# Attention scores that stay in their PSUM banks through a group, moved from key chunk to key chunk by differences of the keys

## The chip, the core and the metric

The kernel runs on one core of one Trainium2 chip. That core has five engines with instruction streams of their own: TensorE (PE in the profile, with PEld for its weight loads), VectorE (DVE), ScalarE (ACT), GpSimd (POOL) and SyncE (SP, which here only issues DMAs). Each works through its stream in order; an instruction waits on semaphores until what it needs is there, and everything behind it on that engine waits too. TensorE writes its results to PSUM, which has eight banks, each of 512 fp32 columns on 128 partitions. The metric is the device time of one execution in microseconds (us).

## What is computed

The input x has 4 sequences of 2048 rows of 256 numbers. With xn = layernorm(x), the output is

```
x + attention(xn) * silu(ffn(xn))
```

```python
q, k, v = xn @ Wq.T + bq, xn @ Wk.T + bk, xn @ Wv.T + bv   # 16 heads of 16 columns
q, k = apply_rope(q), apply_rope(k)                        # rotary positions
att = q . k / 4, masked above the diagonal, softmax over the keys
attention = (att @ v) @ Wo.T + bo
ffn = gelu(xn @ tern(W1).T + b1) @ tern(W2).T + b2          # weights rounded to -1, 0, 1
```

## The kernel before

**Tiling.** The rows are cut into 16 blocks of 512 (four to a sequence; n = block mod 4 is the place in the sequence), the heads into 4 groups of 4. So there are 64 groups (block, head group), worked through in that order. A block of place n sees n + 1 blocks of keys, that is 4(n + 1) key chunks of 128 keys. One key chunk of one group is called a unit here: 4, 8, 12 or 16 units in a group, 640 in all. Heads lie in pairs: one of a pair in partitions 0 to 63, one in 64 to 127. In each half stand 16 dimensions four times, since q and k are both split into a rounded part and a rest (`split`, lines 391 to 397, GpSimd), so that four products add up to nearly full fp32.

**One group** has three parts.

- `maxima` (line 686) takes the scores with queries as rows, 128 queries by up to 512 keys, to find each query's maximum. One step of it is two matmuls (line 704, one for each head of a pair, in two PSUM banks) and two VectorE reductions (line 727, or 731 for the short ones of the diagonal). Blocks of keys on the diagonal get a mask first (line 717). At the end the maxima are negated, turned with a matmul into two banks (line 757) and copied by ScalarE (`mT`, line 765).
- `values` (line 772) takes the scores again with keys as rows. In each unit `scores` runs for the two pairs j = 0, 1: two matmuls of k and q (line 791, part 0), two matmuls that add the negated maxima through a selector (line 791, part 1), one exponential over both banks (line 798, ScalarE), and on the four diagonal units of a group a triangular cut by GpSimd (`affine_select`, line 802). `times_v` (line 813) multiplies with the values, one unit late, so that the exponential of unit u runs beside the products of unit u - 1 with v. Line 815 issues 4 matmuls, each of which shows as two in the profile.
- `end` and `finish` divide by the sums, project, gate with the FFN and store.

**Order.** The schedule is written out by hand (lines 1067 to 1152): while group i runs its units, `maxima` of group i + 1 is advanced by `Paced.to`, half a unit's share before `scores` and half before `times_v`. So on TensorE a full unit reads: a step of maxima, scores, a step of maxima, values. `project` (line 404), which makes q, k and v of a later block, is advanced once a unit over two groups: in the blocks of place 1 and 2 over the groups 0 and 1, in those of place 3 over all four, for two blocks. `feed` (line 566, the FFN) runs at the start of one group in each block, before that group's units.

**PSUM.** Bank 7 belongs to the products with v. The seven others lie in one list (`free_banks`, line 95). `bank` takes the one that has been free longest, `two_banks` the pair of neighbours free longest, `release` puts banks back at the end. The list is worked through while the program is written, so it fixes which bank each instruction uses; on the chip the instruction then waits until the last reader of that bank is done. In `values` a pair is taken for each j and unit, and given back after the exponential.

**project** on GpSimd (on VectorE for the first two blocks): `turn` (line 474) rotates q, then k: six tensor operations and two splits of two operations each, 128 x 512 elements each. The results go to DRAM (`qd`, `kd`, four stores of 512 KB each, line 502), in the stacked order that `maxima` and `values` need. `Loads` (line 615) brings them back by SP: q in 3 buffers, k in 8, v in 5. A tile of k serves `maxima` of a group and then `values` of the same group, which gives it back after the chunk's last scores (line 830).

## Time and profile before

| what | number |
|---|---|
| time, three runs | 2402.01, 2408.93, 2418.55 us (median 2408.93) |
| profiled execution | span 2397.2 us from its first to its last instruction; the page gives no time of its own beyond that |
| median of the runs less the span | 11.7 us |
| granted TensorE clock, mean | 0.986 |
| PE / PEld / DVE / ACT / POOL busy | 95% / 51% / 68% / 61% / 37% of the span |
| DMA | 280.38 MB, mean 117 GB/s; the SP queue's packets take 35.7% of the 16 engines' time |
| line 791, products of k and q | 2560 matmuls, 554.6 us busy |
| line 791, products with the maxima | 2560 matmuls, 516.8 us busy |
| line 704, products for the maxima | 2560 matmuls, 613.0 us busy |
| line 727, reductions of 512 | 1792, 1129.6 us busy |

A matmul's time in the profile is its passage; two matmuls in the two halves of the partitions run beside each other, so how much of TensorE's stream an instruction takes is read from the distance of starts, not from its duration. A PE that is 95% busy is therefore not at its peak. The time before can be told from no change to about 1%.

### The profile page before, as it was taken

The page shows a single profiled execution, that of the slowest core. Times are in us where ns is not written, and L with a number is a line of the kernel's source. Part 1 is how long each engine was busy: PE and PEld are TensorE (multiplying, and loading weights), DVE is VectorE, ACT ScalarE, POOL GpSimd, SP SyncE. Part 2 cuts the span into 40 slices and gives each one's busy share as a digit, 9 for nine tenths or more (in the row PEclk, how much of TensorE's full clock was granted, in tenths as well). Part 3 has the DMA queues.
Part 4 walks back from the last instruction along what each step waited for, and adds up shares of the span by engine and source line. Part 5 has one row for each costly group of instructions (what it writes and reads, how often), then busy time and mean ns, then how long its engine had stood idle before and what let it go on. Part 6 is the DMA issues. An engine that isn't in the chain of part 4 may idle for free.

```text
span 2397.2 us, 43912 instructions
## 1 busy us (share of the span) xinstructions
PE 2269.8 (95%) x16852; PEld 1222.7 (51%) x16852; DVE 1620.1 (68%) x2910; ACT 1472.5 (61%) x1889; POOL 886.6 (37%) x1262
## 2 busy tenths in 40 slices
PE   5799999999999999999999999999999999999997
PEld 4554545545455455544545454455554545455443
DVE  9656677775556676696636768768663766777881
ACT  4554656656766565765766565565676646566665
POOL 2136343235443535315344542522525453431000
PEclk8889999999999999999999999999999999999998
DMA  7344335234253524234234443412514352442311
GB/s 222 113 135 161 92 127 157 58 104 136 75 165 118 178 86 159 79 91 145 67 127 128 151 142 111 155 56 86 176 58 140 120 179 79 135 140 62 88 46 32
DMA packets 247617, 280.38 MB, mean 117 GB/s; under 512 B 108784, under 2 KB 143728, under 8 KB 247408
## 3 DMA queue, kind: packets, MB, share of 16 engines
q1 hardware_dynamic: 243680, 271.95, 35.7%
q10 hardware_dynamic: 3728, 5.64, 0.7%
q8 instruction: 132, 2.16, 0.4%
q14 instruction: 77, 0.63, 0.1%
HBM read 181.08 MB, written 87.52 MB: 112 GB/s over the span
## 4 chain that ended last, share of the span: by engine, by line
PE 71%; DVE 10%; ACT 7%; POOL 6%; issue 3%; DMA 2%; SPq 1%; ACTq 0%; DVEq 0%; POOLq 0%
PE psum L791 19%; PE psum L815 19%; PE psum L704 14%; PE psum L600 5%; PE psum L513 3%; PE psum L581 3%; DVE mx L727 3%; ACT e L798 3%; DVE mx L731 2%; PE psum L539 2%; PE psum L953 2%; PE psum L717 2%; ACT mT L765 1%; POOL qklo L397 1%; ACT g L608 1%
## 5 line engine op out<-in xcount | busy, mean ns | idle before, releaser
L727 DVE TENSOR_REDUCE mx<-psum 128x1 f32<-128x512 f32 (+1 forms) x2048 | 1258.2, 666 | 497.1 <-PE psum L704 350.1
L798 ACT ACTIVATE e<-psum 128x1024 f32<-128x1024 f32 (+3 forms) x1280 | 1081.3, 894 | 630.4 <-PE psum L791 596.0
L704 PE MATMUL psum<-kst,qst 64*128 64x512 f32 (+3 forms) x2560 | 613.0, 421 | 27.1 <-ACT h L592 9.3
L815 PE MATMUL psum<-e,vg 128*32 128x512 f32 (+3 forms) x5120 | 596.5, 543 | 15.7 <-POOL e L802 15.5
L802 POOL TENSOR_SCALAR_AFFINE_SELECT e<-e 128x256 f32<-128x256 f32 x512 | 208.0, 416 | 1001.0 <-ACT e L798 972.2
L791 PE MATMUL psum<-qst,kst 64*128 64x512 f32 (+3 forms) x2560 | 554.6, 395 | 22.3 <-DVE mx L727 5.7
L704 PEld LDWEIGHTS psum<-kst,qst 64*128 64x128 f32 x2560 | 309.0, 185 | 449.4 <-DVE mx L727 287.9
L791 PE MATMUL psum<-mT,sel 64*128 64x512 f32 (+3 forms) x2560 | 516.8, 370 | 6.0 <-ACT mT L765 3.2
L791 PEld LDWEIGHTS psum<-qst,kst 64*128 64x128 f32 x2560 | 285.1, 185 | 171.9 <-ACT e L798 55.4
L791 PEld LDWEIGHTS psum<-mT,sel 64*128 64x128 f32 x2560 | 273.3, 186 | 43.7 <-ACT mT L765 24.1
L594 POOL TENSOR_TENSOR hl<-h,hh 128x512 fp32r<-128x512 f32 x128 | 164.9, 1298 | 149.9 <-ACT h L592 114.3
L815 PEld LDWEIGHTS psum<-e,vg 128*32 128x32 f32 x5120 | 109.9, 108 | 161.0 <-issue 112.4
L731 DVE TENSOR_REDUCE mx<-psum 128x3 f32<-128x384 f32 x256 | 130.3, 552 | 57.7 <-PE psum L717 53.3
L592 ACT ACTIVATE hh<-psum,b1c 128x512 fp32r<-128x512 f32 x128 | 88.4, 691 | 80.4 <-PE psum L581 80.2
L513 PE MATMUL psum<-xf,wqkvT 128*128 128x512 f32 x256 | 125.9, 616 | 0.9 <-ACT xf L458 0.9
L717 PE MATMUL psum<-mask_k,mask_q 64*128 64x64 bf16 (+1 forms) x1536 | 121.1, 205 | 0.0
L600 PE MATMUL psum<-hh,w2T 128*128 128x512 f32 x256 | 107.1, 418 | 0.2 <-ACT w2T L367 0.2
L581 PE MATMUL psum<-xh,w1T 128*128 128x512 f32 x256 | 104.8, 409 | 0.6 <-POOL xh L396 0.5
L581 PE MATMUL psum<-xl,w1T 128*128 128x512 f32 x256 | 103.1, 403 | 0.8 <-POOL xl L397 0.8
L600 PE MATMUL psum<-hl,w2T 128*128 128x512 f32 x256 | 102.3, 399 | 0.2
L521 ACT ACTIVATE qk<-psum,bqk 128x512 f32<-128x512 f32 x64 | 44.0, 689 | 86.4 <-PE psum L513 85.9
L592 ACT ACTIVATE h<-psum,b1c 128x512 f32<-128x512 f32 x128 | 87.9, 687 | 0.0
(135 smaller groups left out, 1635.9 us busy)
## 6 DMA issues: line engine op xcount, KB each, us to landing
kst<-kd SPq DMA_DIRECT2D x160, 512.0 KB
qst<-qd SPq DMA_DIRECT2D x64, 512.0 KB
vg<-vd SPq DMA_DIRECT2D x160, 166.0 KB
qd<-qkhi SPq DMA_DIRECT2D x32, 512.0 KB
qd<-qklo SPq DMA_DIRECT2D x32, 512.0 KB
kd<-qkhi SPq DMA_DIRECT2D x30, 512.0 KB
kd<-qklo SPq DMA_DIRECT2D x30, 512.0 KB
vd<-v SPq DMA_DIRECT2D x16, 574.0 KB
```

Source lines behind the costliest of these rows:

```text
L513: nc.tensor.matmul(pq, wqkvT[:, kc, at : at + P], xf[:, kc, :], start=(kc == 0), stop=(kc == KC - 1),)
L581: nc.tensor.matmul(ph, w1T[:, kc, f * P : (f + 1) * P], x12[:, kc, :], start=(kc + i == 0), stop=(kc + i == KC),)
L592: nc.scalar.activation(to, ph, AF.Gelu, bias=b1c[:, f : f + 1])
L600: nc.tensor.matmul(pgs[dc], w2T[:, f - 2, dc * P : (dc + 1) * P], hx, start=(f - 2 + i == 0), stop=(f - 2 + i == FC),)
L704: nc.tensor.matmul(s1[:, at : at + wt], q[rows, j, t * P : (t + 1) * P], kst[blk, g, c][rows, j, :wt], start=(at == 0), stop=(c < n),)
L717: nc.tensor.matmul(to[:, :, i * ST : (i + 1) * ST], mask_q[rows, i, :], mask_k[rows, i, : len(ts), :], start=False, stop=(i == 1),)
L727: nc.vector.tensor_reduce(mx[:, 2 * j + a, at : at + 1], s1[:, :w], AX.X, ALU.max)
L731: nc.vector.tensor_reduce(mx[:, 2 * j + a, at : at + w // P], s1[:, :w].rearrange("p (b k) -> p b k", k=P), AX.X, ALU.max,)
L791: nc.tensor.matmul(s2[:, a, :w], (k, sels[j][rows, :])[part], (q[rows, j, q0:], mT[rows, q0:])[part], start=(part == 0), stop=(part == 1),)
L798: nc.scalar.activation(e, s2[:, :, :w], AF.Exp, scale=1.0 / math.sqrt(HD))
L802: nc.gpsimd.affine_select(out=e[:, :, :P], in_=e[:, :, :P], pattern=[[0, 2], [1, P]], compare_op=ALU.is_ge, fill=0.0, base=0, channel_mult ...
L815: nc.tensor.matmul(av[h * HP : (h + 1) * HP, q0:], vst[blk, g, kb // TT][:, kb % TT, h * VE : h * VE + HP], ex[h // 2][:, h % 2, : NB - q0 ...
```

## The change

The scores of a pair j stay in one fixed pair of banks (0, 1 for j = 0; 2, 3 for j = 1) through all units of a group. The first unit writes the product of q and the first key chunk plus the negated maxima, as before. Each later unit adds the product of q with the differences d = (keys of this chunk) - (keys of the chunk before), which turns the scores of the one chunk into those of the next. The products with the maxima are issued in the first unit only.

- `project` makes the differences, splits them and stores them (`steps_of_keys`, four stores of 512 KB to `sd`). It has one yield more, so `N_Q` is one higher. The rotated k is kept in `turned_k` with the last 128 columns of the block before.
- The halves hi and lo now come from a pool of two buffers of half the size, one taken by q, k and d each.
- `Loads` has a fourth kind, d, with 3 buffers and one group ahead. k is used by `maxima` alone, has 4 buffers, and is given back there.

```diff
+    def pair_of_banks(name, i):
+        free_banks.remove(i)
+        free_banks.remove(i + 1)
+        taken.setdefault(name, []).append([i, i + 1])
+        return psum[:, i : i + 2, :]
...
+    turned_k = const.tile([P, 2, P + NB], F32, name="turned_k")
+    nc.gpsimd.memset(turned_k[:, :, :P], 0.0)
...
-    kp = ctx.enter_context(tc.tile_pool(name="kp", bufs=8))
+    kp = ctx.enter_context(tc.tile_pool(name="kp", bufs=4))
+    dp = ctx.enter_context(tc.tile_pool(name="dp", bufs=3))
...
+    halfp = ctx.enter_context(tc.tile_pool(name="halfp", bufs=2))
...
+        def halved(hi, lo, full):
             if not start:
-                split(hi[:, 2 * i, :], lo[:, 2 * i, :], r0, (NB,))
+                split(hi, lo, full, (NB,))
             else:
-                nc.scalar.copy(hi[:, 2 * i, :], r0)
+                nc.scalar.copy(hi, full)
+                eng.tensor_tensor(lo, full, hi.bitcast(F32), ALU.subtract)
+
+        def stacked(dd, hi, lo, rows):
             for c, src in enumerate(rows):
...
+                queue = nc.scalar if blk == 0 and dd is not qd else nc.sync
+                queue.dma_start(out=to[c], in_=src.bitcast(F32))
...
+        def steps_of_keys():
+            hi, lo = halves()
+            for s in range(2):
+                d = one.tile([P, NB], F32, tag=f"r{s}", name=f"d{s}")
+                eng.tensor_tensor(
+                    d, turned_k[:, s, P:], turned_k[:, s, :NB], ALU.subtract
+                )
+                halved(hi[:, s, :], lo[:, s, :], d)
+            if n + 1 < NQ:
+                eng.tensor_copy(turned_k[:, :, :P], turned_k[:, :, NB:])
+            else:
+                eng.memset(turned_k[:, :, :P], 0.0)
+            stacked(sd, hi, lo, (hi, lo, hi, lo))
...
             while pairs and (blk or i):
                 turn(*pairs.pop(0))
+        steps_of_keys()
+        yield
...
-            self.free = {"q": 3, "k": 8, "v": 5}
+            self.free = {"q": 3, "k": 4, "d": 3, "v": 5}
...
-            self.ahead = {"q": 2, "k": 2, "v": 1}
+            self.ahead = {"q": 2, "k": 2, "d": 1, "v": 1}
...
+        def d(self, blk, g, c):
+            t = dst[blk, g, c] = dp.tile([P, 2, NB], F32R, tag="dst", name="dst")
+            nc.sync.dma_start(
+                out=t.bitcast(F32),
+                in_=sd[blk - blk % NQ + c][2 * g : 2 * g + 2].rearrange("r p k -> p r k"),
+            )
...
+                if ts[-1] == (TT - 1 if c < n else 0) and j == GH // 2 - 1:
+                    kst.pop((blk, g, c))
+                    loads.release("k")
...
+        banks = [pair_of_banks("s2", 2 * j) for j in range(GH // 2)]
         def scores(kb, j, q0):
-            s2 = two_banks("s2")
+            s2 = banks[j]
...
-            for part in range(2):
+            for part in range(1 if kb else 2):
                 for a in range(2):
                     rows = slice(a * ST, (a + 1) * ST)
-                    k = kst[blk, g, kb // TT][rows, j, (kb % TT) * P : (kb % TT + 1) * P]
+                    d = dst[blk, g, kb // TT][rows, j, (kb % TT) * P : (kb % TT + 1) * P]
                     nc.tensor.matmul(
-                        s2[:, a, :w],
-                        (k, sels[j][rows, :])[part],
+                        s2[:, a, q0:],
+                        (d, sels[j][rows, :])[part],
                         (q[rows, j, q0:], mT[rows, q0:])[part],
-                        start=(part == 0),
-                        stop=(part == 1),
+                        start=(kb == 0 and part == 0),
+                        stop=(kb > 0 or part == 1),
+                        skip_group_check=True,
                     )
-            nc.scalar.activation(e, s2[:, :, :w], AF.Exp, scale=1.0 / math.sqrt(HD))
-            release("s2")
+            nc.scalar.activation(e, s2[:, :, q0:], AF.Exp, scale=1.0 / math.sqrt(HD))
+            if kb == last:
+                release("s2")
...
             if kb % TT == TT - 1:
-                kst.pop((blk, g, kb // TT))
-                loads.release("k")
+                dst.pop((blk, g, kb // TT))
+                loads.release("d")
```

## The prediction

> **What bounds the kernel now.** I read the page first: the busy shares, the chain that ended last, the groups.
>
> ```profile
> span 2397.2 us, 43912 instructions
> PE 2269.8 (95%) x16852; PEld 1222.7 (51%) x16852; DVE 1620.1 (68%) x2910; ACT 1472.5 (61%) x1889; POOL 886.6 (37%) x1262
> ...
> PE 71%; DVE 10%; ACT 7%; POOL 6%; issue 3%; DMA 2%; SPq 1%; ACTq 0%; DVEq 0%; POOLq 0%
> ...
> L727 DVE TENSOR_REDUCE mx<-psum 128x1 f32<-128x512 f32 (+1 forms) x2048 | 1258.2, 666 | 497.1 <-PE psum L704 350.1
> ```
>
> TensorE carries 71% of the chain; line 791, half of which goes, has 19% of the span there. VectorE comes next, and its 68% is an average, so I went to the timeline of a stretch with nothing but attention in it (a group of place 3, in the second sequence):
>
> ```profile
> 1197.52 0.50 PE L704 MATMUL psum<-kst,qst 64*128 64x512 f32 x2
> 1197.85 0.40 PE L791 MATMUL psum<-qst,kst 64*128 64x512 f32 x2
> 1198.05 2.51 DVE L727 TENSOR_REDUCE mx<-psum 128x1 f32<-128x512 f32 x4 [1.19 <-PE psum L704]
> 1198.09 0.40 PE L791 MATMUL psum<-mT,sel 64*128 64x512 f32 x2
> 1198.32 0.41 PE L791 MATMUL psum<-qst,kst 64*128 64x512 f32 x2
> 1198.55 0.41 PE L791 MATMUL psum<-mT,sel 64*128 64x512 f32 x2
> 1198.59 1.94 ACT L798 ACTIVATE e<-psum 128x1024 f32<-128x1024 f32 x2 [0.41 <-PE psum L791]
> 1198.78 0.51 PE L704 MATMUL psum<-kst,qst 64*128 64x512 f32 x2
> 1199.22 1.06 PE L815 MATMUL psum<-e,vg 128*32 128x512 f32 x8
> 1200.21 0.51 PE L704 MATMUL psum<-kst,qst 64*128 64x512 f32 x2
> 1200.58 0.50 PE L791 MATMUL psum<-qst,kst 64*128 64x512 f32 x2
> 1200.75 4.00 DVE L727 TENSOR_REDUCE mx<-psum 128x1 f32<-128x512 f32 x6 [0.19 <-PE psum L704]
> ```
>
> From scores to scores (1197.85 to 1200.58) a unit takes 2.73 us. Each pair of matmuls of line 791 holds TensorE for 0.23 us. VectorE has two steps of maxima a unit, four reductions, 2.51 us. TensorE is the bound here with VectorE 0.2 us behind; ScalarE needs 1.94.
>
> The second place is POOL's 6%. The chain of waits shows where it lies, in the second group of a block of place 1:
>
> ```profile
> 785.55 1.29 POOL qklo L397
> ...
> 804.48 1.27 POOL qklo L397
> 805.95 0.34 POOL e L802
> 806.33 1.41 PE psum L815 x8
> ```
>
> Between these lines stands nothing but GpSimd's `turn`; the triangular cuts queue behind it, and TensorE waits (the timeline puts 1.50 us of idle time ahead of the matmul at 806.33).
>
> **What goes.** In every unit but a group's first, the two pairs with the maxima: 2304 matmuls. With 0.23 us a pair of 512 columns, 0.46 a unit, there are 448 full units less 64 first ones, 384 x 0.46 = 177 us. The narrow diagonal units (0.34, 0.24, 0.20 by their starts) give 64 x 0.78 = 50. Together 227 us, 9% of the span.
>
> **What takes it back: the banks left for the maxima.** Four of seven banks now belong to `values`; three remain for the two of each step of maxima and for all else. In a ring of three, the second matmul of a step can start only when the first reduction of the step before is done. That takes 0.53 us from issue to the start of the reduction (1197.52 to 1198.05), 0.68 for the reduction (the groups by shape: 1792 of 512 columns with a mean of 683 ns; 0.63 apart when they follow closely), and some 0.06 to the next matmul (a reduction ended at 909.83 elsewhere, the weight load behind it began at 909.89): 1.27 us. In the timeline over the whole run, 447 of the 576 changed units stand between two steps of maxima. For the full ones the distance of these steps has a median of 1.38 us (middle eight tenths 1.26 to 1.65); without the 0.46 it would be 0.9 to 1.0, so the wait puts back most. Clipped at 1.27 unit by unit, these give 44 us instead of about 160; the other 129 units give their full 41. Where a unit then has no maxima it is held by ScalarE's 1.94; I take off 6. **Gain 79 us**, bounds 0 and 150 (the upper if VectorE's 2.51 were the only limit: 0.23 in each of 344 full units, 79, plus 41 and some 30 for narrow ones and first steps).
>
> On the banks that stay: the page "PSUM — Partial Sum Buffer" of the Trainium skill, in its "Summary: rules for kernel authors", advises that TensorE write a different bank from the one being read, which speaks against this change. Taken bare it would add a wait of an exponential, 0.97 us, to each of 1152 pairs. Here the first exponential ends at 1199.56, the next product for its banks is due at 1200.5; the second at 1200.53, its product due 0.23 later, so I cost this at nothing.
>
> **What is added.**
>
> - GpSimd, 14 blocks: two subtractions of 1.28 us (row of line 479), two splits of 1.04 to 1.09 and 1.28 (lines 396, 397) and a copy of 256 elements (0.4 by the triangular cut's row, 0.7 by half a subtraction): 7.9 us, issued straight behind k's `turn`. In the place shown above nothing hides it: 4 x 7.9, and what TensorE gained in that group is lost in the wait, 3 more: **35 us**. In blocks of place 2 GpSimd idles 4.57 us before the next cut, so some 2 us stick out; in place 3's last group 9.4 us of idle time are cut down by the faster units, some 3 to 4 us stick out: together **17**. Bounds of all GpSimd terms 25 and 70.
> - `mT`. The two banks of line 757 now belong to the three. The next step of maxima comes right behind it 47 times of 64, takes one of these banks, and waits for ScalarE's copy; before, only the product with the maxima waited, with that step and the first product in the gap:
>
> ```profile
> 1217.19 0.43 PE L757 MATMUL psum<-id_half,m_pad 64*68 64x64 f32 x8
> 1217.46 0.47 PE L704 MATMUL psum<-kst,qst 64*128 64x512 f32 x2
> 1217.85 0.48 PE L791 MATMUL psum<-qst,kst 64*128 64x512 f32 x2
> 1217.89 0.57 ACT L765 CAST mT<-psum 68x512 fp32r<-68x512 f32 x1
> 1218.51 0.50 PE L791 MATMUL psum<-mT,sel 64*128 64x512 f32 x2 [0.18 <-ACT mT L765]
> ```
>
>   0.34 + 0.23 us of cover, 47 times: **27 us**, bounds 0 and 36.
> - Two steps of maxima back to back (some 16 a sequence, 0.2 to 0.9 us apart now) are pushed to 1.27. Most lie in groups where VectorE is 85 to 88% busy and would end no sooner; I count a third, 5 us a sequence: **20**, bounds 0 and 60.
> - `project` keeps one bank for v over a yield, one or two units long; then the maxima have two banks and the second matmul waits for the second reduction, 0.63 more, some 6 units a sequence outside the GpSimd wait: **14**, bounds 0 and 25.
> - SP and DMA: 160 loads and 64 stores of 512 KB, 280 to about 398 MB. SP is in order, so loads behind the d stores wait for GpSimd. The first d tile of a new sequence is released 8 units before use, behind those stores: 3 us, three times, **10**, bounds 0 and 40. Other d tiles are asked for 8 units (20 us) ahead and hide; k has a group's time.
> - Start: 3.1 us of VectorE (five operations of about 0.69 to 0.3) for each of blocks 0 and 1, and four more DMA issues on ScalarE: **6**, bounds 2 and 10.
>
> The sum: 79 - 35 - 17 - 27 - 20 - 14 - 10 - 6 = -50. The span goes from 2397 to about 2447; with the 11.7 us between span and median, 2459. The waits hide a little in one another, so I say **2455 us**, 1.9% slower.
>
> **The rivals.**
>
> 1. *Faster: VectorE becomes the bound, and the three banks don't bind.* For it: seven banks, of which four were nearly always with the scores, held up the maxima's weight loads already (287.9 us of such waits, mostly behind work that had to be done anyway), so three may be as good. Then the gain is 150, the steps back to back and the v banks cost nothing, and GpSimd 52, `mT` 0 to 27, loads 10 and start 6 remain: 55 to 82 us faster, about 2340. It decides from a distance of steps around the scores below about 1.15 us: each 0.1 there is worth some 40 us.
> 2. *No difference.* The gain is nearer 100 and a third of the waits lie in each other's shade: 2409, within 1%.
> 3. *Much slower: lockstep.* TensorE waits for VectorE at every second step, VectorE then for TensorE, which is in order and stuck behind values; back-to-back steps cost 60, the v banks 25, the loads 40, GpSimd 70: gain 60 less 231, some 2560 at the far end, 2510 as its near edge. Against it: a step's two reductions leave 1.25 us of work while TensorE passes from one step to the next.
> 4. *The change doesn't take effect*, with the scores rewritten each unit: the diff issues part 1 in the first unit alone, so I give it no chance of its own.
>
> **How the numbers follow.** Forecast (slower, 2434 to 2510) 0.47; rival 1 0.28; rival 2 0.16; rival 3 0.09. A measurement of this kernel can tell about 1% from no change, 2385 to 2433. So faster 0.28, same 0.16, slower 0.56. The range leaves out most of rival 3 and the lower third of rival 1: 2325 to 2515; the forecast's own range is 2434 to 2510.
>
> **What would show it.** In the changed profile: TensorE's matmuls 16852 - 2304 = 14548, its busy time well below 2270. A full unit's steps of maxima around the scores 1.2 to 1.3 us apart, with waits of line 704 on VectorE; units of about 2.6 us. In place 1's second group TensorE idle for about 8 us ahead of the products with v, released by the triangular cut. GpSimd near 1000 us. A step of maxima behind line 757 waiting for `mT`. DMA near 398 MB, and waits for d tiles only at the start of a sequence. I am wrong if the steps come closer than 1.15 us, if units fall to 2.5 us (rival 1), or if the units grow beyond 2.73 (rival 3).

## The result and the profile after

The changed kernel takes **2525.82 us** (median of four runs, 2521.97 to 2530.63), the kernel before beside it 2407.07 us: 1.049 times as long, 95% interval 1.0457 to 1.0523. The forecast was 2455 us with a range to 2515. The side was right, the size was not: the loss is 119 us by the medians and 126.7 us in the profiled spans (2397.2 to 2523.9), where the prediction had 50.

The page of the changed kernel; the lines of the code have moved: the products for the maxima are L750 (704 before), their reductions L773 and L777 (727, 731), the turning of the maxima L806 (757), the scores L844 (791), the cut L857 (802), the products with v L870 (815).

```profile
span 2523.9 us, 39667 instructions
PE 2222.9 (88%) x14548; PEld 1080.4 (43%) x14548; DVE 1620.4 (64%) x2920; ACT 1469.7 (58%) x1893; POOL 986.1 (39%) x1361
...
PE 55%; DVE 21%; POOL 11%; ACT 5%; DMA 4%; issue 3%; SPq 1%; ACTq 0%; POOLq 0%; DVEq 0%
...
L773 DVE TENSOR_REDUCE mx<-psum 128x1 f32<-128x512 f32 (+1 forms) x2048 | 1252.3, 666 | 594.6 <-PE psum L750 404.7
```

The 2304 products are gone (16852 - 14548), but TensorE's busy time fell by 47 us only, not by the 227 they were counted at; 197 us of it now fall into stretches at half clock (below), where 47 us did before. Its part of the chain went from 71% to 55%, VectorE's from 10% to 21%, GpSimd's from 6% to 11%. The mean granted clock fell from 0.986 to 0.946.

TensorE's waits in the changed kernel (line, what it waited for: total us, times, longest):

```profile
PE psum L844 <- DVE mx L773: 58.4, 41, 5.9
PE psum L870 <- POOL e L857: 44.9, 15, 8.6
PE psum L750 <- DVE mx L773: 36.5, 103, 3.1
PE psum L750 <- DVE mx L777: 23.5, 46, 9.8
...
PE psum L844 <- DMA dst<-sd: 12.5, 3, 5.3
```

The first line is one that the prediction doesn't have: scores that wait for a reduction of the maxima. Before, that wait was 5.7 us in all. The second is the wait for GpSimd that was predicted.

Where the scores wait so is seen in the timeline around the start of a group (the first block of the third sequence):

```profile
1343.31 0.43 PE L806 MATMUL psum<-id_half,m_pad 64*68 64x64 f32 x8 [0.56 <-DVE m_pad L797]
...
1343.58 0.48 PE L750 MATMUL psum<-kst,qst 64*128 64x512 f32 x2
...
1344.17 1.29 DVE L773 TENSOR_REDUCE mx<-psum 128x1 f32<-128x512 f32 x2 [0.91 <-PE psum L763]
...
1345.51 0.80 PE L844 MATMUL psum<-qst,dst 64*128 64x512 f32 x2 [1.38 <-DVE mx L773]
...
1346.10 0.63 PE L844 MATMUL psum<-mT,sel 64*128 64x512 f32 x2
...
1346.53 0.63 PE L844 MATMUL psum<-qst,dst 64*128 64x512 f32 x2
```

The group before has just given back banks 0 to 3. The list hands banks out in the order of their return and stands at 4, 0, 1, 2, 3, 5, 6 here (the turned maxima had 5 and 6), so the step of maxima at 1343.58 takes banks 4 and 0. The new group must have banks 0 to 3 and no others, so its first scores wait until the second reduction of that step, which reads bank 0, is done (1344.17 + 1.29 = 1345.46), 1.38 us idle. By the program's list, the step just ahead has a bank of the first scores in 45 of the 64 groups. The second thing to see are the distances after it: matmuls that follow one another in 0.23 us elsewhere stand 0.43 apart (1346.10 to 1346.53). TensorE runs at half its clock here.

The trace's record of the granted clock has the half clock in pieces of 3.41 us. Stretches of it: 11 before, 69 us in all; 42 in the changed kernel, 277 us. In 21 of the 42 the longest idle time of TensorE that began in the 7 us ahead is such a wait at the start of a group, 1.33 to 1.38 us long. The Trainium skill, "TensorE: Matmul & The Clock Gate", section "HAM oscillation — how this bites in real kernels", gives the rule as no idle gaps above about 3.4 us. Here 10 of the 42 stretches have an idle time above 3.4 us there; the other 32 have only shorter ones.

A steady stretch of the changed kernel, place 3 of the second sequence, answers to the prediction's first timeline:

```profile
1268.41 0.50 PE L750 MATMUL psum<-kst,qst 64*128 64x512 f32 x2
...
1268.75 0.62 PE L844 MATMUL psum<-qst,dst 64*128 64x512 f32 x4
1268.94 2.48 DVE L773 TENSOR_REDUCE mx<-psum 128x1 f32<-128x512 f32 x4 [0.22 <-PE psum L750]
...
1269.21 0.97 PE L750 MATMUL psum<-kst,qst 64*128 64x512 f32 x2
...
1269.69 0.18 PEld L750 LDWEIGHTS psum<-kst,qst 64*128 64x128 f32 x1 [0.52 <-DVE mx L773]
...
1270.11 1.06 PE L870 MATMUL psum<-e,vg 128*32 128x512 f32 x8
...
1271.45 0.62 PE L844 MATMUL psum<-qst,dst 64*128 64x512 f32 x4
```

From scores to scores it is 2.70 us, where 2.73 stood before: 0.46 us of products are gone from this unit, and it became 0.03 shorter. The second matmul of the step behind the scores waits for the first reduction of the step ahead of them (weight load at 1269.69), and the products with v start at 1270.11, 1.70 us behind the first step. Before, they started at 1199.22, also 1.70 us behind the first step at 1197.52.

### The profile page after: what moved, and what is told of

It reads as the page before. It is cut to its first block, busy times and chain, and to the rows that moved or that the text cites. A ratio compares the mean times of both kernels' runs of the same rounds, so it can differ in the third digit from the quotient of the medians.

```text
span 2523.9 us, 39667 instructions
## 1 busy us (share of the span) xinstructions
PE 2222.9 (88%) x14548; PEld 1080.4 (43%) x14548; DVE 1620.4 (64%) x2920; ACT 1469.7 (58%) x1893; POOL 986.1 (39%) x1361
## 2 busy tenths in 40 slices
DMA packets 308530, 397.57 MB, mean 158 GB/s; under 512 B 112368, under 2 KB 147312, under 8 KB 308336
## 4 chain that ended last, share of the span: by engine, by line
PE 55%; DVE 21%; POOL 11%; ACT 5%; DMA 4%; issue 3%; SPq 1%; ACTq 0%; POOLq 0%; DVEq 0%
PE psum L870 16%; PE psum L750 15%; DVE mx L773 13%; PE psum L844 6%; PE psum L638 5%; PE psum L619 4%; PE psum L549 3%; DVE mx L777 3%; POOL lo L410 2%; PE psum L763 2%; POOL hi L409 2%; PE psum L577 2%; PE psum L1008 1%; DMA dst<-sd 1%; ACT e L852 1%
## 5 line engine op out<-in xcount | busy, mean ns | idle before, releaser
L773 DVE TENSOR_REDUCE mx<-psum 128x1 f32<-128x512 f32 (+1 forms) x2048 | 1252.3, 666 | 594.6 <-PE psum L750 404.7
L750 PE MATMUL psum<-kst,qst 64*128 64x512 f32 (+3 forms) x2560 | 754.5, 442 | 95.8 <-DVE mx L773 36.5
L870 PE MATMUL psum<-e,vg 128*32 128x512 f32 (+3 forms) x5120 | 615.7, 559 | 45.0 <-POOL e L857 44.9
L750 PEld LDWEIGHTS psum<-kst,qst 64*128 64x128 f32 x2560 | 331.4, 189 | 655.3 <-DVE mx L773 483.8
L857 POOL TENSOR_SCALAR_AFFINE_SELECT e<-e 128x256 f32<-128x256 f32 x512 | 204.6, 410 | 1016.6 <-ACT e L852 984.5
L844 PE MATMUL psum<-qst,dst 64*128 64x512 f32 (+3 forms) x2560 | 450.3, 403 | 89.0 <-DVE mx L773 58.4
L844 PEld LDWEIGHTS psum<-qst,dst 64*128 64x128 f32 x2560 | 242.1, 193 | 217.4 <-ACT e L852 75.9
L870 PEld LDWEIGHTS psum<-e,vg 128*32 128x32 f32 x5120 | 114.4, 112 | 189.6 <-issue 114.0
L777 DVE TENSOR_REDUCE mx<-psum 128x3 f32<-128x384 f32 x256 | 130.8, 552 | 55.5 <-PE psum L763 51.1
L763 PE MATMUL psum<-mask_k,mask_q 64*128 64x64 bf16 (+1 forms) x1536 | 135.8, 208 | 0.0
L549 PE MATMUL psum<-xf,wqkvT 128*128 128x512 f32 x256 | 126.7, 622 | 0.9 <-ACT xf L471 0.9
L763 PEld LDWEIGHTS <-mask_q 64*128 64x128 bf16 x1536 | 67.8, 98 | 34.8 <-issue 19.9
```

What stands on the lines that cost most here:

```text
L549: nc.tensor.matmul(pq, wqkvT[:, kc, at : at + P], xf[:, kc, :], start=(kc == 0), stop=(kc == KC - 1),)
L750: nc.tensor.matmul(s1[:, at : at + wt], q[rows, j, t * P : (t + 1) * P], kst[blk, g, c][rows, j, :wt], start=(at == 0), stop=(c < n),)
L763: nc.tensor.matmul(to[:, :, i * ST : (i + 1) * ST], mask_q[rows, i, :], mask_k[rows, i, : len(ts), :], start=False, stop=(i == 1),)
L773: nc.vector.tensor_reduce(mx[:, 2 * j + a, at : at + 1], s1[:, :w], AX.X, ALU.max)
L777: nc.vector.tensor_reduce(mx[:, 2 * j + a, at : at + w // P], s1[:, :w].rearrange("p (b k) -> p b k", k=P), AX.X, ALU.max,)
L844: nc.tensor.matmul(s2[:, a, q0:], (d, sels[j][rows, :])[part], (q[rows, j, q0:], mT[rows, q0:])[part], start=(kb == 0 and part == 0), stop ...
```

## The experiments

All times are medians in us; the ratio is to runs of the kernel before on the same chip (medians 2406 to 2411). The last column counts the stretches of half clock in the profiled execution and their sum.

| kernel | time | ratio, 95% interval | half clock |
|---|---|---|---|
| changed kernel | 2525.8 | 1.0490 (1.0457 to 1.0523) | 42, 277 us |
| banks_alone | 2473.7 | 1.0261 (1.0230 to 1.0291) | 30, 156 |
| banks_free | 2392.0 | 0.9931 (0.9912 to 0.9950) | 16, 103 |
| keep_banks | 2499.2 | 1.0384 (1.0351 to 1.0417) | 37, 244 |
| free_choice | 2443.6 | 1.0143 (1.0107 to 1.0180) | 23, 165 |
| zero_products | 2523.2 | 1.0471 (1.0435 to 1.0507) | 32, 211 |
| no_differences | 2475.7 | 1.0278 (1.0245 to 1.0311) | 39, 206 |
| steps_vector | 2680.9 | 1.1127 (1.1097 to 1.1157) | 47, 393 |
| later_steps | 2514.8 | 1.0436 (1.0400 to 1.0472) | 36, 189 |
| after_half_reduce | 2378.1 | 0.9876 (0.9839 to 0.9914) | 35, 216 |
| before_half_reduce | 2380.6 | 0.9878 (0.9852 to 0.9905) | 16, 108 |
| before_longer_mt | 2507.8 | 1.0414 (1.0387 to 1.0441) | 34, 169 |
| one_pair | 2561.9 | 1.0626 (1.0591 to 1.0660) | 40, 267 |
| one_pair_keep | 2502.3 | 1.0395 (1.0354 to 1.0436) | 18, 154 |
| one_pair_free | 2518.7 | 1.0460 (1.0424 to 1.0495) | 20, 169 |
| one_pair_best | 2457.6 | 1.0201 (1.0166 to 1.0236) | 16, 128 |
| two_pairs_best | 2461.9 | 1.0210 (1.0178 to 1.0243) | 39, 233 |
| free_later | 2406.0 | 1.0000 (0.9985 to 1.0015) | 21, 138 |
| free_later_start | 2397.8 | 0.9964 (0.9949 to 0.9980) | 21, 135 |

In what follows a group's length is the distance of the copies of `av`, summed over the four sequences.

### 1. The banks alone

`banks_alone`: the kernel before, with the fixed pairs and nothing else. All products stay, and there are no differences.

```diff
+        banks = [pair_of_banks("s2", 2 * j) for j in range(GH // 2)]
...
-            s2 = two_banks("s2")
+            s2 = banks[j]
...
-            release("s2")
+            if kb == last:
+                release("s2")
```

> The kernel before with one part of the change alone: each pair j keeps its two fixed banks (0, 1 and 2, 3) through a group and gives them back after its last unit; scores are still written anew in every unit, no differences, no new loads, no new GpSimd work. Theory 1 (the allocation of the banks is a main cost: first scores of a group wait for whoever used banks 0 to 3 last, and the maxima have three banks): 45 to 90 us slower than before, 2450 to 2500, with waits of the scores on VectorE at most group starts and a lower granted clock. Theory 2 (GpSimd's added work, its stores and the late loads are the main cost): 2395 to 2420, as before.

Measured 2473.65 us, 65 us more than the kernel before. So more than half of the loss comes with the allocation of the banks, before any product is taken away or any difference made. How it comes about, this run doesn't say: the number of rotating banks and the fixed choice change together here.

### 2. What the differences cost, and where

`steps_vector`: the changed kernel with the subtractions, splits and copies of `steps_of_keys` on VectorE.

```diff
-                eng.tensor_tensor(
+                nc.vector.tensor_tensor(
                     d, turned_k[:, s, P:], turned_k[:, s, :NB], ALU.subtract
                 )
-                halved(hi[:, s, :], lo[:, s, :], d)
+                if not start:
+                    nc.vector.tensor_copy(hi[:, s, :], d)
+                    nc.vector.tensor_tensor(
+                        lo[:, s, :], d, hi[:, s, :].bitcast(F32), ALU.subtract
+                    )
+                else:
+                    halved(hi[:, s, :], lo[:, s, :], d)
...
-                eng.tensor_copy(turned_k[:, :, :P], turned_k[:, :, NB:])
+                nc.vector.tensor_copy(turned_k[:, :, :P], turned_k[:, :, NB:])
```

> The changed kernel with the differences of the keys made on VectorE instead of GpSimd in every block (seven operations of 0.3 to 0.7 us in place of 7.9 us on GpSimd). Theory 2 (GpSimd's chain in the second group of place 1, where that group got 10.4 to 11.7 us longer): those four groups fall back to about 38 us, 30 to 45 us gained, 2480 to 2495. Rival (that group is long because of the banks or the clock): 2515 to 2530.

Measured 2680.94 us: 155 us more than the changed kernel, far from either expectation. VectorE's own waits in this run say why:

```profile
DVE d L532 <- POOL turned_k L515: 74.1, 14, 10.2
...
DVE d L532 <- POOL turned_k L519: 47.1, 14, 3.7
```

The first subtraction of each block stands in VectorE's stream and waits up to 10.2 us for GpSimd's `turn`. The reductions stand behind it, and behind them the steps of maxima, which have three banks: the waits of their products for reductions of 512 go from 36.5 to 157.4 us. The experiment measured a wait ahead of a crowded queue, not the work, and so tells nothing of the cost on GpSimd. I hadn't asked what stands behind the moved instruction.

`no_differences`: the computation is left out; the keys are stored a second time, so the transfers stay.

```diff
                 stacked(kd, hi, lo, (hi, lo, hi, lo))
+                stacked(sd, hi, lo, (hi, lo, hi, lo))
...
-        steps_of_keys()
         yield
...
-                        start=(kb == 0 and part == 0),
+                        start=(part == 0),
```

> The changed kernel without the computation of the differences: the keys themselves are stored a second time in their place, with the same transfers, and each chunk's product starts its bank afresh, so that the scores lack the maxima after the first chunk. It measures what the 75 to 80 us of GpSimd work, and the work on VectorE and ScalarE in the start, cost on the path. Theory: place 1's second group loses 31 of its 44 us, the start some 10 of 24, together 2465 to 2490 us. Rival: the second group of place 1 is slow for the want of banks and not for GpSimd's chain: 2505 to 2525 us.

Measured 2475.73 us: the differences cost 50 us. By groups: the second groups of place 1 go from 197.3 to 161.7 us (before: 152.9), block 0 from 197.4 to 186.2 (before: 173.5). Place 2 doesn't move (687.3 and 687.9), place 3 gives 5.5.

`later_steps`: nothing left out, the differences of blocks 1 to 15 made piece by piece beside the next FFN stage.

```diff
+        if blk:
+            later.append(
+                steps_of_keys(nc.gpsimd, lambda hi, lo, full: split(hi, lo, full, (NB,)))
+            )
...
                 for k, _ in enumerate(gate):
...
+                    if later:
+                        next(later[0], None)
```

> The changed kernel, with the differences of blocks 1 to 15 computed in small pieces beside the next FFN stage and not in the projection; nothing is left out. If GpSimd's chain ahead of the causal selects is what place 1's second group waits for, that group returns to the 167 us (four sequences) that it took with the banks alone changed, and the whole takes 2480 to 2500 us. Rival: GpSimd is as late in the FFN stage, where the split of h waits behind the pieces: 2515 to 2545 us.

Measured 2514.84 us. The second groups of place 1 went to 157.7 us, below even the run with the banks alone (166.6). So the chain on GpSimd was most of what they had lost. But the time came back in the FFN stages, as the rival said:

```profile
PE psum L648 <- POOL hl L642: 39.7, 30, 1.5
```

L648 are the products with W2, which wait for the split of h behind the pieces.

### 3. What the removed products were worth

`zero_products`: the changed kernel with a second product for each chunk that adds zeros.

```diff
-            for part in range(1 if kb else 2):
+            for part in range(2):
...
-                        (d, sels[j][rows, :])[part],
+                        (d, m_pad[rows, 0, MP:] if kb else sels[j][rows, :])[part],
```

> The changed kernel, with a second product per chunk put back that adds nothing (60 columns of zeros with the row of maxima; 64 of 448 of them were there as real ones). It measures what taking the products away is worth inside the changed kernel. If the steps of the maxima ring through three banks set the pace there, as the prediction's 79 of 227 us says, the time is 2570 to 2620 us. Rival: the products were worth their full length, and the losses elsewhere are larger than thought: 2700 us or more. Second rival: beside three banks they were only filling time in which TensorE now waits, and kept its clock up: 2500 to 2550 us.

Measured 2523.22 us, against 2525.82 without these products: **2304 matmuls are put back and the time doesn't change.** TensorE is busy 2295.5 us instead of 2222.9, and waits that much less. A pair of them holds TensorE for 0.23 us at the median, as the real ones did. This is the experiment that overturns the prediction's largest term. The second rival held: in the whole, the products only filled time in which TensorE now waits. By places (one profile of each kernel) it is not zero everywhere: places 2 and 3 take 1518.3 us with the products and 1506.5 without, places 0 and 1 985.7 with them and 995.9 without, and there the half clock is 52 us longer without them.

`after_half_reduce` and `before_half_reduce` say what it waits for. Both take the maximum of a tile of queries over half the columns of the bank, so half the keys are left out of the maxima.

```diff
-                            mx[:, 2 * j + a, at : at + 1], s1[:, :w], AX.X, ALU.max
+                            mx[:, 2 * j + a, at : at + 1], s1[:, : w // 2], AX.X, ALU.max
```

> The changed kernel, with the maxima of one tile of queries taken over half the columns of the bank only (half the keys are left out of the maxima; the products are all there). A reduction of 0.67 us becomes about 0.4 us, VectorE does some 530 us less, and the round through the three banks is 0.5 us shorter. If that round holds TensorE in the changed kernel: 2380 to 2450 us. Rival: TensorE is held by its own clock and by the starts of the groups, which wait less by the same 0.5 us only: 2480 to 2520 us.

> The kernel before, with the same reductions cut to half the columns (half the keys are left out of the maxima). In the changed kernel this cut was worth 147 us. If the reductions are on the path there only because three banks are left for them, the kernel before, whose steps have up to seven, gains little: 2360 to 2410 us. Rival: VectorE is as much on the path of the kernel before, and the three banks have no part in it: 2260 to 2310 us.

Measured: the changed kernel falls by 148 us to 2378.08 (2 us below its range), the kernel before by 30 us to 2380.58. The windows show it best in a stretch of attention alone (place 3 of the second sequence, third group, 16 units): the stretch, its length, then the busy time of PE, PEld, DVE, ACT and POOL, the clock, DMA's share and GB/s. The kernel before:

```profile
1176.25:1220.93 44.68, 44.38 (x356) 22.15 (x356) 32.73 (x60) 31.18 (x38) 11.06 (x25) 1.00 0.26 77
```

The kernel before with the short reductions:

```profile
1159.37:1203.71 44.34, 44.12 (x356) 21.26 (x356) 21.29 (x59) 31.19 (x38) 11.05 (x25) 1.00 0.27 77
```

The changed kernel:

```profile
1246.20:1290.58 44.38, 41.33 (x298) 17.53 (x298) 33.28 (x61) 30.95 (x38) 10.98 (x25) 0.96 0.40 126
```

The changed kernel with the short reductions:

```profile
1172.11:1212.81 40.70, 38.88 (x298) 16.65 (x299) 21.21 (x60) 30.87 (x39) 11.01 (x25) 1.00 0.41 127
```

Before, TensorE is busy throughout (44.38 of 44.68), and shorter reductions change 0.3 us. In the changed kernel the length is nearly the same, TensorE has 3 us of holes, and shorter reductions take 3.7 us off. The pace went from TensorE to the round of a step through three banks and VectorE, and that round is nearly as long as what TensorE needed before. Two other things are in the 44.38 us: 3.4 us at half clock (the 0.96) and, near the end, the next group's first scores with a wait of 1.36 us. With the choice of banks free (part 5) the same group takes 42.26 us in `free_choice` and, with all products, 44.09 in `banks_free`. So 1.8 us of the 6.3 that this group's products were counted at (12 x 0.46 + 0.78) can be had.

### 4. What a wait of TensorE costs

`before_longer_mt`: the kernel before, with ScalarE's copy of the turned maxima issued three times, so that the first product with them waits longer, 64 times by 1.16 us, 74 us.

```diff
+        for _ in range(2):
+            nc.scalar.copy(
+                mT[:MP].rearrange("p (t a k) -> p a t k", a=2, k=ST),
+                pt[:MP, :, : TT * ST].rearrange("p a (t k) -> p a t k", k=ST),
+            )
```

> The kernel before with the copy of mT issued three times, so that TensorE waits 1.16 us longer at the start of each of the 64 groups and for nothing else. If a wait costs its own length: 74 us at most, 2460 to 2481. If waits of this size bring on half-clock stretches of 3.4 us and more, as the clock's mean of 0.946 in the changed kernel suggests: more than 74 us, 2490 to 2560, with a granted clock below 0.97. If other work hides it: under 40.

Measured 2507.84 us: 99 us for 74 us of copies. The half clock grew from 69 to 169 us, and matmuls at half clock stand twice as far apart (0.43 for 0.23 us above). In the profiles TensorE idles 65 us more than in the kernel before, and 96 us more of its busy time fall into half clock, which makes up to 48 us lost. That is 113 us together, where the spans differ by 108: the clock is enough for the difference of 25. The run doesn't separate it from what else is late behind the copies; the waits of L704 for ScalarE's FFN work, for one, grew from 9.3 to 18.7 us.

### 5. The fixed choice of banks

`keep_banks`: the changed kernel, but banks 0 to 3 are given back only ahead of an FFN stage.

```diff
-        banks = [pair_of_banks("s2", 2 * j) for j in range(GH // 2)]
+        if not held:
+            held.extend(pair_of_banks("s2", 2 * j) for j in range(GH // 2))
+        banks = list(held)
```

> The changed kernel, but banks 0 to 3 are not given back between groups, only ahead of an FFN, so that the steps of maxima at the end and start of a group can't take them. Theory 1 (41 waits of the first scores on VectorE, 1.4 us each, and the slower clock behind them): 40 to 70 us gained, 2455 to 2485, and the waits of the scores' matmuls on the reductions of 512 fall from 58 us to under 15. Rival (the first step of maxima now waits for the copy of mT as long instead): 2515 to 2530.

Measured 2499.18 us, 27 us less than the changed kernel, between the theory and its rival. The wait of the scores for reductions of 512 falls from 58.4 to 16.3 us, but steps of maxima and FFN products now wait for the copy of mT (13.1 and 10.2 us), and the trailing steps of a group and the two banks of the turned maxima now also share the three banks that are left.

`one_pair`: half of the change. Pair 0 of a group stays in banks 0 and 1 and adds differences; pair 1 is computed afresh in rotating banks, with its own tiles of k.

```diff
+            if j:
+                s2 = two_banks("s1p")[:, :, :w]
+                tile, fresh = lst, True
+            else:
+                s2 = held_pair[:, :, q0:]
+                tile, fresh = dst, kb == 0
...
-            for part in range(1 if kb else 2):
+            for part in range(2 if fresh else 1):
```

> Half of the change: only the first pair of heads of a group keeps its scores in two fixed banks and adds differences; the second pair is computed afresh from its keys for every chunk, with the product that subtracts the maxima, in banks that rotate. Five banks rotate in place of three; GpSimd's work stays whole. If the number of rotating banks is what costs, most of the 65 us that the fixed banks cost alone go, and half of the removed products (114 us) has some room to be a gain: 2390 to 2470 us. Rival: any bank fixed through a group costs as much, by the forced choice at the start of a group: 2490 to 2540 us.

Measured 2561.93 us, 36 us *more* than the whole change and above both ranges. My theory, that the number of rotating banks is what costs, had 2390 to 2470 and fell here. TensorE's waits in this run:

```profile
PE psum L849 <- DVE mx L773: 67.2, 62, 5.9
...
PE psum L750 <- ACT e L857: 17.9, 33, 1.2
```

41 of the 62 waits of scores (L849) stand at the start of a group and take 58.7 us; in the whole change it was 41 and 58.4 us. The other 21 lie within groups, and steps of maxima wait for exponentials, since the second pair moves through their banks. In all TensorE idles even less than in the whole change (262 us for 297), but half of the products are back. Why they cost time here, where all of them cost none in `zero_products`, stays open.

`two_pairs_best` and `one_pair_best` join `keep_banks` with a second repair: the differences of the block that is projected in place 1 are made in five pieces beside the first chunks of place 1's third group.

```diff
+        later.append(steps_of_keys())
+        if n != 2:
+            for _ in later.pop():
+                pass
...
                 next(steps)
+                for _ in range(2 if later and n == 1 and g == 2 else 0):
+                    next(later[0], None)
```

> The changed kernel with two repairs: banks 0 to 3 are given back only ahead of an FFN stage, and the differences of the block that is projected in place 1 are computed in five pieces beside the first chunks of place 1's third group. The first repair took 27 us alone; the second should take the 31 us that the second group of place 1 lost to GpSimd's chain. If the two are separate costs: 2455 to 2475 us. Rival: the pieces are late in the third group, as they were in the FFN stage: 2490 to 2510 us.

> Half of the change, as above, with the same two repairs. By the same terms it gains 30 to 45 us on the kernel with half of the change alone: 2360 to 2430 us. Rival: GpSimd's work and the half change hold it at 2450 us or more.

Measured 2461.93 and 2457.64 us. The first is as expected: the two repairs add up (27 and 37 us), and place 1's second groups take 155.8 us in place of 197.3. The second missed its range by 28 us and lies where the rival had it, though the repairs took 104 us from half of the change.

`one_pair_keep`, `free_choice` and `one_pair_free` separate the two repairs and test the choice itself. In the latter two the banks are still held through a group and returned at its end, but the pairs are not fixed:

```diff
-    def pair_of_banks(name, i):
+    def pair_of_banks(name):
+        when = {i: k for k, i in enumerate(free_banks)}
+        i = min(
+            (i for i in (0, 2, 4) if i in when and i + 1 in when),
+            key=lambda i: max(when[i], when[i + 1]),
+        )
```

> Half of the change, with banks 0 and 1 given back only ahead of an FFN stage, and GpSimd's pieces left in the projection. Half of the change took 2562 us; with both repairs 2458. If it is the return of the banks at the end of a group, and the forced taking of the same banks at the start of the next, that made half of the change slower than the whole: 2485 to 2505 us, and 30 to 45 us of the 104 are left for GpSimd's pieces. Rival: GpSimd's pieces were most of the 104: 2530 us or more.

> The changed kernel, with the two pairs of a group chosen at its start among banks 0-1, 2-3 and 4-5, those first that were given back longest ago; everything else as changed. Four banks are held through a group as before, three rotate. If the wait at the start of a group comes from the fixed choice of banks 0 to 3, which the step just issued has taken: 2490 to 2505 us, as with the banks kept (2499). Rival: any four banks are as late, since three rotate beside them: 2515 to 2535 us.

> Half of the change, with the one pair of a group chosen in the same way, not fixed. If the fixed choice is what costs there too: 2480 to 2510 us, within 15 us of the kernel that keeps its pair. Rival: 2545 us or more.

Measured 2502.26, **2443.64** and 2518.66 us. The first is as expected; the third, 43 us below the fixed pair, is 9 us above its range and 16 us above the kernel that keeps its pair. Seven lines of choice take 82 us from the changed kernel, more than keeping the banks did, and more than I expected. The start of the same group there (TensorE's timeline; here L849 are the scores, L755 the products for the maxima, L811 the turning of the maxima):

```profile
1306.97 0.43 PE L811 MATMUL psum<-id_half,m_pad 64*68 64x64 f32 x8 [0.56 <-DVE m_pad L802]
1307.23 0.48 PE L755 MATMUL psum<-kst,qst 64*128 64x512 f32 x2
1307.56 0.23 PE L768 MATMUL psum<-mask_k,mask_q 64*128 64x64 bf16 x4
1307.62 0.47 PE L849 MATMUL psum<-qst,dst 64*128 64x512 f32 x2
1308.08 0.50 PE L849 MATMUL psum<-mT,sel 64*128 64x512 f32 x2
1308.41 0.39 PE L849 MATMUL psum<-qst,dst 64*128 64x512 f32 x2
1308.64 0.40 PE L849 MATMUL psum<-mT,sel 64*128 64x512 f32 x2
```

The scores follow the step at once (0.39 us behind it, where 1.93 us stood), and the matmuls keep their full pace (1308.41 to 1308.64). By the program's list the step just ahead never has a bank of the first scores now. In all the wait of scores for reductions falls from 58.4 to 0.2 us, and the half clock from 277 to 165 us. Since other waits grew a little, TensorE idles 45 us less in all, and 94 us less of its busy time fall into half clock, worth up to 47 us: 92 together, where the spans differ by 83.

`banks_free`: the same choice in the kernel of `banks_alone`, without any other part of the change.

> The kernel before with two pairs of banks held through a group, nothing else of the change, as in banks_alone (2474 us), but with the pairs chosen among banks 0-1, 2-3 and 4-5, those given back longest ago. If what the banks cost is the fixed choice at the start of a group, and three rotating banks would do: 2400 to 2425 us. Rival: three rotating banks cost by themselves, and the choice mattered only beside the other parts: 2450 us or more.

Measured 2391.97 us, 8 us below the range, where the fixed choice took 2473.65. The scores' 50.8 us of waits for reductions of 512 are gone, and the half clock falls from 156 to 103 us. So **three rotating banks cost this kernel nothing; the fixed choice cost all of it**, 82 us here as in the changed kernel. It is even 0.7% faster than the kernel before (0.9931, 0.9912 to 0.9950). Why was not tried.

`free_later` joins the free choice with the repair of place 1, `free_later_start` also moves the differences of blocks 0 and 1 to GpSimd, their stores to SyncE, and spreads those of block 1 over block 0's groups:

```diff
-                queue = nc.scalar if blk == 0 and dd is not qd else nc.sync
+                queue = nc.scalar if blk == 0 and dd is kd else nc.sync
...
         def steps_of_keys():
+            eng = nc.gpsimd
...
-        if n != 2:
+        if n != 2 and blk != 1:
```

> The changed kernel with the pairs chosen so (2444 us alone), and the differences of the block that is projected in place 1 computed beside place 1's third group. If GpSimd's chain still costs place 1's second group 30 to 37 us: 2403 to 2417 us, no difference from the kernel before that can be told. Rival: with the choice free the chain is hidden otherwise: 2430 us or more.

> The same, with the differences of blocks 0 and 1 computed on GpSimd and not on VectorE and ScalarE, their stores issued by SyncE and not by ScalarE, and those of block 1 spread over block 0's groups. Block 0 took 20 us more than in the kernel before; if 10 to 18 of them come from that work in the start: 2388 to 2405 us, as fast as the kernel before or up to 1% faster. Rival: the start is late for other reasons: within 5 us of the run without this repair.

Measured 2405.98 and 2397.84 us, both as expected. In place 1 the second groups take 153.4 us (152.9 before). The last repair takes 8 us, all in block 0 (192.6 to 184.9; before 173.5).

With three repairs the change is 0.4% faster than the kernel before (0.9964, 0.9949 to 0.9980), but slower than `banks_free`, which keeps all products and makes no differences. Of all kernels here that leave nothing out, that one is the fastest.

## Why the prediction was wrong

**The step that failed most is one that it doesn't have: the forced choice of banks at the start of a group, 82 us.** I read the change's banks as a number, "three remain", and asked how a ring of three turns. That a fixed number of the bank also fixes *when* it must be free, against a list that hands out just these banks to the step before, I didn't see, although the diff shows both functions. The prediction came closest at `mT`: it has the step behind the turned maxima wait for ScalarE's copy, 47 times, 27 us, for want of another bank. In the changed kernel there is no such wait, since at that moment banks 0 to 3 are in the list. In most groups the step takes the last of the three and one of these, and the scores pay. Only where the banks are kept (`keep_banks`, and here `two_pairs_best`) does the profile show the wait that I described, 12.4 us at the maxima and 9.7 us at the FFN.

**The gain, 79 us, was nothing in the whole.** `zero_products` gives -3 us with an uncertainty of some 12. The round of three banks was priced rightly: 1.27 us by the prediction, 1.28 in the steady unit (the second matmul's weight load at 1269.69, the first step at 1268.41), and in that unit, where the steps stood 1.26 us apart before, no gain is what the clip gives. It holds for the whole run. In the 327 full units between two steps, the first product of the step ahead and the second product of the step behind are 1.28 us apart at the median, and 1.28 in `banks_free` with all products too (1.50 before). The first products of the two steps did come closer, to 0.81 us. So the prediction's own sign of being wrong, steps less than 1.15 us apart, came, but without rival 1's gain, since the step waits at its second product. (Before, this distance has a median of 1.28 us in the count over the trace, not 1.38 as the prediction read it; the clip gives 46 us there, about its 44.)

What failed is the reading of the other units. I took whatever their steps stood further apart than 1.27 us for time of the products, so for removable, and gave the units without two steps around them their full 0.46. From the products with v of one unit to those of the next, full units with one step ahead of the scores and one behind (some 270) have a median of 2.87 us before, 2.77 in `banks_free` and in `zero_products`, both with all products, 2.77 in `free_choice` and 2.73 in the changed kernel, both without them. So at most 0.04 of the 0.46 was there to be had, and 0.10 came from elsewhere. (With the short reductions it is 2.44.) The 12 us that places 2 and 3 gain are lost again in places 0 and 1. There the changed kernel has 52 us more of half clock than with the products put back, with 41 us more of TensorE's busy time in it, worth up to 21 us; that this is the reason was not tried. With the choice of banks free, places 2 and 3 together take 1469.4 us in `free_later` and 1472.9 in `banks_free`, where all products stand: 3.5 us of gain, after what the differences still cost there.

**The half clock was no term at all.** The sum counted each wait at its length. In `before_longer_mt` 74 us of copies ahead of TensorE cost 99, and the changed kernel runs 277 us at half clock instead of 69. The granted clock of 0.986 stood in the profile before; I took it for a constant.

**GpSimd: right in the place, too high elsewhere.** Place 1's second groups: predicted 35 us; with the choice of banks free, 189.8 less 153.4 us without the chain there, 36. The chain of the changed kernel shows it as it was described:

```profile
855.93 1.22 POOL d L532
...
862.02 1.26 POOL lo L410
863.28 0.34 POOL turned_k L537
...
863.82 0.34 POOL e L857
...
864.20 2.28 PE psum L870 x8
```

From the first subtraction to the copy's end it is 7.7 us (predicted 7.9), and TensorE idles 8.56 us in front of the products at 864.20 (predicted about 8). Places 2 and 3 were to lose 17 us; without the differences they take 5 less.

**The start was too cheap at 6 us.** Block 0 lost 24 us. Taking away the differences gives 11 of them, freeing the choice of banks 4; 8 come back when the work leaves VectorE and ScalarE. What remains was not separated.

**Loads: right.** Predicted 10 us at the first d tile of three sequences; measured three waits of L844 for d tiles, 12.5 us, the longest 5.3. DMA moves 397.57 MB (398 predicted), and no other wait for a d tile is in the list.

**Steps back to back and the bank of v, 20 and 14 us,** can't be judged singly. The waits of L750 for reductions grew from 8.2 us (4.7 and 3.5) to 60.0, but in `zero_products` they are 24.4 at the same time of the whole, so they aren't losses.

**The rivals.** The time fell into the numbers of rival 3 (2510 to 2560), but not by its mechanism: the steady unit didn't grow, it went from 2.73 to 2.70 us, and no lockstep is in the timeline. (Its far end of 2560 doesn't follow from its own sum, which gives 2409 + 231 - 60 = 2580.) The loss lies at the starts of groups, in place 1 and in the start of the kernel. Rival 1's condition, that three banks don't bind, holds for the cost of the banks (`banks_free`) and fails for the gain. The page "PSUM — Partial Sum Buffer" of the Trainium skill, in its "Summary: rules for kernel authors", advises another bank for the matmul than the one being read. I cost that at nothing against the trace: `banks_free` writes each unit's scores into the banks that the last exponential has read, and its scores wait 2.7 us for exponentials in all, 4.0 before. In the changed kernel it is 8.6 us in 31 waits, so the term was small, but not nothing.

## What to carry to other kernels

A bank, buffer or register that is named and not chosen must be free at one moment. Ask who holds it just then; a list that is worked through in turn may have handed it to the step right in front. When work is taken from the engine that sets the pace, find the next round behind it and ask, unit by unit, what else fills the time that the work seems to take: here 9% of the span could be taken out and put back without a change of the time. And a wait of TensorE is to be counted above its length where the granted clock falls behind it.

## What the hardware showed that I had not expected

- Idle times of TensorE of 1.33 to 1.38 us, with small matmuls around them, began ahead of 21 of 42 stretches at half clock, which come in pieces of 3.41 us. Taking away the waits at the starts of groups alone left 23 stretches (165 us in place of 277).
- TensorE's busy time says little of its work: 2304 matmuls more are 72.6 us more of busy time at the same span.
- A kernel that holds four of seven banks through a group, with the choice free, is 0.7% faster than one in which all seven rotate; its full units take 2.77 us at the median, not 2.87.
